# Block fusion on TensorE through diagonal matrices, a larger GpSimd share of the state input product, and two attention steps half a slot away from their old places

## The chip, the cores and the metric

The kernel runs on one core of a Trainium2 chip. The metric is the device time of one execution in microseconds. The core has five engines that run side by side, each through its own instructions in order, and that meet through semaphores: TensorE (PE in the profile; its weight loads are PEld), VectorE (DVE), ScalarE (ACT), GpSimd (POOL) and SyncE (SP), which here issues the DMAs.

## The reference, cut to what matters

The input x has 8 samples of 512 channels by 48 x 48 positions, read as 2304 steps of a sequence, all in fp32. Two layers follow each other.

- Layer 0: group norm, then causal linear attention with 8 heads of 64 channels and features elu + 1; the numerator is divided by the product of Q with the running sum of K; the result is added to x.
- Layer 1: group norm, then four groups of 128 channels, one after the other. Each group runs a Mamba block (projection, convolution over 4 steps, a selective scan with 256 inner channels and 16 states, gating, projection back), and its output is fused with its input. The fused result is added to the input of the next group:

```python
for i in range(4):
    x_i = spx[i] + prev if prev is not None else spx[i]
    x_m = mamba(x_i)
    fused_global = maximum(x_i, x_m)
    w_local, w_global = sigmoid(mean(x_i)), sigmoid(mean(fused_global))
    fused = w_local * x_i + w_global * fused_global
    feats.append(fused); prev = fused
```

The means run over all positions, so a group must be finished before its fusion can start. The concatenated `feats` are added to the input of layer 1. "Block fusion" below means the line of `fused`, and the sum that makes the next group's `x_i`.

## The kernel before

**Blocks, jobs, slots.** A block is one group of one sample (32 blocks). Two streams (`streams[0]` with the even samples, `streams[1]` with the odd ones) take turns block by block, so that the fusion and the preparation of one stream's next block happen while the other stream's block is scanned. A block has 6 chunks of 384 steps (`LC`), each a `Job` of 8 slots (`SLOTS`): 2 halves of the inner channels (`h`) by 4 sets of states (`q`). This makes 1536 slots.

**One slot.** `slot(k)` emits the product of B with delta times x for the next slot, four decays (`decay`, L885, Exp on ScalarE, from SBUF into a PSUM bank), four scans on VectorE (`scan`, L895, which read that bank and the product and write `u`), the weighting by C on GpSimd (`weigh`, L908), and the sum over states on TensorE (`gather`, L922, into the bank `yp`). The product is shared: `product` (L875, VectorE) does the columns 0 to `LC - TAIL` of each of 4 row groups, reading B from PSUM, where ScalarE has copied it (`inputs`, L848, `Bp`); `last_product` (L864, GpSimd, emitted two slots ahead) does the last `TAIL` columns, reading B from SBUF. `TAIL` is 128. `u` has 5 buffers. Scans release their banks in program order, and up to three decays (`DEPTH`) are emitted ahead of the scans while banks are free. Six PSUM banks (`spare`) serve the decays and everything else but `yp` and `Bp`.

**The order of the rest.** All engines' programs are written out by one planner. Work beside the scans is a set of generators (`Task`); each `yield when, banks` says from which half slot on, and with how many free PSUM banks, it goes on. `beside(half)` runs twice per slot: half 2k ahead of the slot's first scan, and half 2k + 1 after its second. It first steps the attention tasks (`heads`) that need no bank, then `tasks` (fusion, preparation, finish of a job), then `heads` again. Since the same things come back every job, a period is 8 slots or 16 halves; below, "half 7" means half 7 of such a period.

**Attention** is a second pipeline, `chunk(m)`: one chunk of 384 steps of two heads (`o` is the pair of heads) per period, started at half 3 (`times[m]`, then `at(j)` is j halves later). It projects q (half 3), k (5) and v (7) at L300, each four products; ScalarE makes Exp (L312) and Relu (L313), and VectorE the features q (L359, half 5) and k (L367, half 7). At half 8 TensorE sums k along the sequence (`kc`, L373, plus the sum kept from the pass before, L375, where `o` is not 0), VectorE multiplies with q (`pr`, L386, half 10), and ScalarE copies v and kc (L378, L382, half 9). The states and denominators follow (L405 to L423, half 15); `rd` is 1/denominator (L433), `rdb` its broadcast (L441). In the next period TensorE transposes `rdb` (L445, `at(16)`, half 3), VectorE scales q with it (L450, half 5), TensorE makes the scores of two heads (L457, L467, half 6), ScalarE takes their masked part by a Relu into `sm` (L479, `at(21)`, half 8), TensorE makes the output (L484 to L498, half 9), ScalarE copies it out (L508, half 11). With `o` 0, GpSimd also normalises the input, four times L324.

**Preparation of a job** (`prepare`): convolution (L707) at halves 11 and 13, gate (L718), Silu (L743 to L748) at half 14, then B, C and delta go through DRAM and come back spread over partitions (L797 to L812). GpSimd makes `dx` (L819). The finish of a job, two slots into the next, is `yz` on VectorE (L934), the projection (L940) at half 4, and the maximum (`fg`, L951).

**Fusion** is `Stream.pass_on`. `wt` holds the two sigmoid weights, `xi` the stream's current `x_i` for all steps, `fu` the loaded maximum, `xb` the next group's slice of layer 1's input, `xa` (tile `xo`) the old group's slice. `loads(c)` loads the three. For each chunk ScalarE scales `fu` and `xi` (L668, L669) and normalises `xb` (L673), GpSimd adds `fu` and `xi` (L676), and then `xb`, into `xi` (L681); a third addition makes the output (L684). When the next group belongs to a new sample (`self.fresh`), there is no L681, and ScalarE normalises straight into `xi` (L679). The tasks are placed at 33 and 25 half slots ahead of the job that needs them, the first chunk of a block as soon as its norm is known.

Of the kernel before, what the change touches and what calls it, by code (L numbers as in the profile page):

```python
# [9 lines left out]
F32 = mybir.dt.float32  # L10
BF16 = mybir.dt.bfloat16
AF = mybir.ActivationFunctionType
ALU = mybir.AluOpType
# [4 lines left out]
P = 128  # L18
T = 128
LC = 384  # L20
NI, NQ, NGR = 4, 4, 4
SLOTS = 8
TAIL = 128
BANKS = 6
DEPTH = 3
LEAD = 11
# [23 lines left out]
def attention_then_mamba_kernel(  # L50
# [12 lines left out]
    nc = tc.nc  # L63
    B, _, L = x.shape
    NS = 16
    NC = L // LC
# [6 lines left out]
    small = ctx.enter_context(tc.tile_pool(name="small", bufs=2))  # L73
# [7 lines left out]
    ident = cst[:, C_ID : C_ID + P]  # L81
# [198 lines left out]
    def chunk(m):  # L280


        b, o, c = parts[m]
        n = f"{b}_{o}_{c}"
        bank = Banks()
        NT = LC // T
        cols, tile_rows = slice(c * LC, (c + 1) * LC), slice(o * P, (o + 1) * P)
# [3 lines left out]
        def at(j, gap=1):  # L291
            return times[m] + j, gap
# [23 lines left out]
        if o == 0:  # L316
# [3 lines left out]
            xn, norm = fetched.pop(m), norms[b]  # L320
# [85 lines left out]
        more = NT if c + 1 < NC else NT - 1  # L406
# [4 lines left out]
        if c:  # L411
# [4 lines left out]
                start=True,  # L416
                stop=False,
                skip_group_check=True,
            )
        for i in range(more):  # L420
            for j in range(i + 1):
                for h in heads_of:
# [16 lines left out]
        yield at(15), 0  # L439
        rdb = new("rdb", 1, (P, 2 * NT, 64))  # L440
        nc.scalar.copy(rdb, rd.unsqueeze(2).to_broadcast([P, 2 * NT, 64]))  # L441
        yield at(16), 1
        rb = bank()[:, 0:LC].rearrange("p (i t) -> p i t", i=NT)
        for i in range(NT):
            nc.tensor.transpose(  # L445
# [10 lines left out]
        for sc in scs:  # L456
# [4 lines left out]
                start=True,  # L461
                stop=False,
                skip_group_check=True,
            )
        for i in range(NT):
            for h, sc in zip(heads_of, scs):
# [4 lines left out]
                    start=False,  # L471
                    stop=i == NT - 1,
                    skip_group_check=True,
                )
        yield at(21), 0
        sms = []
        for par, sc in enumerate(scs):
            sm = new(f"sm{par}", 1, (P, NT, T))
# [43 lines left out]
    class Stream:  # L522
# [55 lines left out]
        def pass_on(self):  # L578


            xi = self.xi
            old = None
            if self.b is not None:
                old = self.b, self.s, self.n, self.fm
                wt = small.tile([P, 4], F32, tag="wt", name=f"wt_{self.n}")
                nc.vector.tensor_copy(wt[:, 2:3], self.sums)
                nc.vector.tensor_reduce(wt[:, 3:4], self.fsum, AX.X, ALU.add)
            last = old is not None and old[1] == 3 and not self.samples
            if old is not None:
                yield "1", 0  # L590
                nc.scalar.activation(wt[:, 0:2], wt[:, 2:4], AF.Exp, scale=-1.0 / L)
                yield "1", 0
                nc.vector.tensor_scalar_add(wt[:, 0:2], wt[:, 0:2], 1.0)
                nc.vector.reciprocal(wt[:, 0:2], wt[:, 0:2])
            if not last:
                self.move_on()
                while (self.b, self.s) not in done:
                    yield "1w", 0
                norm = done[self.b, self.s]
            s = self.s  # L600
            if not last:
# [12 lines left out]

            def loads(c):
                fu = xb = xa = None
                cols = slice(c * LC, (c + 1) * LC)
                if not last:
                    xb = mpool.tile([P, LC], F32, tag="xb", name=f"xb_{self.n}_{c}")
                    nc.sync.dma_start(out=xb, in_=x1s[self.b][s * P : (s + 1) * P, cols])  # L620
                if old is not None:
                    fu = mpool.tile([P, LC], F32, tag="fu", name=f"fu_{old[2]}_{c}")
                    nc.sync.dma_start(out=fu, in_=old[3][:, cols])
                    xa = mpool.tile([P, LC], F32, tag="xo", name=f"xo_{old[2]}_{c}")
                    nc.sync.dma_start(out=xa, in_=x1s[old[0]][old[1] * P : (old[1] + 1) * P, cols])
                return fu, xb, xa

            if last and self.z:

                got = [  # L630
                    mpool.tile([P, 4, 1 + LC], F32, tag="u", name=f"end_{i}", bufs=5)
                    for i in range(NC // 2)
                ]
                for c in range(NC):
                    fu, xa = (got[c // 2][:, c % 2 * 2 + i, 0:LC] for i in range(2))
                    cols = slice(c * LC, (c + 1) * LC)
                    rows = slice(old[1] * P, (old[1] + 1) * P)
                    nc.sync.dma_start(out=xa, in_=x1s[old[0]][rows, cols])
                    nc.sync.dma_start(out=fu, in_=old[3][:, cols])
                for c in range(NC):  # L640
                    fu, xa = (got[c // 2][:, c % 2 * 2 + i, 0:LC] for i in range(2))
                    cols, icols = slice(c * LC, (c + 1) * LC), slice(3 + c * LC, 3 + (c + 1) * LC)
                    for t, i in ((xi[:, icols], 0), (fu, 1)):
                        nc.vector.scalar_tensor_tensor(
                            xa, t, wt[:, i : i + 1], xa, ALU.mult, ALU.add
                        )
                    nc.sync.dma_start(out=out[old[0], rows, cols], in_=xa)
                return
            now = loads(0)
            for c in range(NC):  # L650

                if c and not last:
                    first = 2 * self.jobs[self.block * NC + c].start
                    yield (first - 33, 1), 0
                    now = loads(c)
                    yield (first - 25, 1), 0
                elif c:
                    yield "3", 0
                    now = loads(c)
                    yield "1", 0  # L660
                else:
                    yield "1", 0
                cols, icols = slice(c * LC, (c + 1) * LC), slice(3 + c * LC, 3 + (c + 1) * LC)
                fu, xb, xa = now
                if not last:
                    normed = dict(bias=norm[:, 1, :], scale=norm[:, 0, :])
                if old is not None:
                    nc.scalar.activation(fu, fu, AF.Copy, scale=wt[:, 1:2])  # L668
                    nc.scalar.activation(xi[:, icols], xi[:, icols], AF.Copy, scale=wt[:, 0:1])  # L669
                if old is None:  # L670
                    nc.scalar.activation(xi[:, icols], xb, AF.Identity, **normed)
                elif not last and not self.fresh:
                    nc.scalar.activation(xb, xb, AF.Identity, **normed)  # L673
                if old is not None:
                    yield "1", 0
                    nc.gpsimd.tensor_tensor(fu, fu, xi[:, icols], ALU.add)  # L676
                    yield "2" if c and self.fresh and not last else "1", 0
                    if not last and self.fresh:
                        nc.scalar.activation(xi[:, icols], xb, AF.Identity, **normed)  # L679
                    elif not last:  # L680
                        nc.gpsimd.tensor_tensor(xi[:, icols], xb, fu, ALU.add)  # L681
                    self.ready = c + 1
                    yield "1", 0
                    nc.gpsimd.tensor_tensor(xa, xa, fu, ALU.add)  # L684
                    save(out[old[0], old[1] * P : (old[1] + 1) * P, cols], xa)
                self.ready = c + 1

    class Job:

# [281 lines left out]
    for n in range(4 * NC * B):  # L971
        block, c = n // NC, n % NC
# [121 lines left out]
    def at(k):  # L1094
        return jobs[k // SLOTS], k % SLOTS
# [198 lines left out]
```

## Time and profile before

| what | value |
|---|---|
| median of 3 runs | 8326.95 us (8322.77 to 8327.64) |
| profiled execution, its own time | 8326.65 us |
| its span, first to last instruction | 8324.9 us |
| mean granted TensorE clock | 0.931 |
| first scan starts, last scan starts | 193.3, 8300.7 us |
| busy: PE, DVE, ACT, POOL | 7181.1, 7964.6, 7076.7, 7756.5 us |

The span is what the profile's shares refer to; the profiled execution's own time lies 1.75 us above it. In a group of instructions the columns are: line, engine, operation, output <- inputs, shapes, count, then the busy time of the group in us, the mean length of one in ns, and the idle time of the engine ahead of them with what ended most of it. Successive instructions of VectorE overlap by some tens of ns, so busy time over count is less than the mean length. An fp32 matmul has two records. A line of the waits reads: who waited for whom, us in total, times, longest.

### The profile page before, as it was taken

What the parts mean: (1) busy time and instruction counts of PE and PEld (TensorE: products, weight loads), DVE (VectorE), ACT (ScalarE), POOL (GpSimd) and SP (SyncE); (2) the same over time, 40 slices, a digit from 0 to 9 for tenths busy, and PEclk for the clock granted to TensorE, in tenths of its full rate; (3) what the DMA queues carried; (4) which work ended last, traced back from release to release, by engine and by line L of the source; (5) the groups of instructions that cost most, each with busy time, mean ns of one, the idle gap of its engine ahead of it and who ended that gap; (6) DMA issues with size and microseconds to landing.
All of it is one profiled execution on the core that took longest, in us unless ns stands there. A gap on an engine that the chain in (4) does not pass through costs nothing.

```text
span 8324.9 us, 131321 instructions
## 1 busy us (share of the span) xinstructions
PE 7181.1 (86%) x38850; PEld 3392.3 (41%) x38850; DVE 7964.6 (96%) x10534; ACT 7076.7 (85%) x15014; POOL 7756.5 (93%) x4235
## 2 busy tenths in 40 slices
PE   8888888888888888888888888888888888888864
PEld 4444444443344444444444444444434444444421
DVE  3999999999999999999999999999999999999998
ACT  3888888888888888888888888888888888888886
POOL 2989999999999999999999999999999999999998
PEclk9999999999899999999999999999999999999976
DMA  6777878877777887787777778887777777777765
GB/s 202 194 188 200 210 205 206 206 194 202 205 199 200 204 206 206 198 204 197 202 205 200 199 205 208 205 201 195 203 202 205 201 193 201 203 198 196 190 169 145
DMA packets 1097343, 1654.89 MB, mean 199 GB/s; under 512 B 143913, under 2 KB 989353, under 8 KB 1096498
## 3 DMA queue, kind: packets, MB, share of 16 engines
q1 hardware_dynamic: 1096626, 1646.48, 76.9%
q8 instruction: 309, 5.06, 0.3%
q14 instruction: 408, 3.34, 0.1%
HBM read 1318.23 MB, written 327.68 MB: 198 GB/s over the span
## 4 chain that ended last, share of the span: by engine, by line
DVE 30%; ACT 24%; PE 14%; DMA 14%; issue 10%; POOL 5%; SPq 3%; ACTq 0%; DVEq 0%; POOLq 0%
DVE u L895 20%; PE bank L300 9%; ACT bank L885 8%; DVE u L875 6%; POOL u L908 3%; DMA dxr<-xscr 3%; ACT L885 2%; DMA dr<-dscr 2%; DMA B<-scr 2%; ACT L743 2%; DMA xo<-x 2%; ACT L778 1%; PE bank L718 1%; SPq L810 1%; SPq L797 1%
## 5 line engine op out<-in xcount | busy, mean ns | idle before, releaser
L895 DVE TENSOR_TENSOR_SCAN u<-bank,u 128x385 f32<-128x385 f32 (+1 forms) x6144 | 5442.9, 938 | 110.7 <-ACT bank L885 109.1
L908 POOL TENSOR_TENSOR u<-u,C 128x1536 f32<-128x1536 f32 x1536 | 4890.4, 3184 | 365.7 <-DVE u L895 203.7
L885 ACT ACTIVATE bank<-dr,scales 128x385 f32<-128x385 f32 (+1 forms) x6144 | 3399.5, 579 | 558.6 <-DVE u L895 532.1
L864 POOL TENSOR_TENSOR u<-B,dxr 128x512 f32<-128x512 f32 x1536 | 1966.1, 1280 | 28.0 <-DMA ksum<-before 15.4
L300 PE MATMUL bank<-xn,wq 128*128 128x384 f32 x4608 | 1946.3, 573 | 36.5 <-DVE u L895 14.5
L875 DVE TENSOR_TENSOR u<-Bp,dxr 128x1024 f32<-128x1024 f32 x1536 | 1842.9, 1200 | 15.0 <-ACT Bp L848 9.5
L922 PE MATMUL yp<-u,cst 128*32 128x384 f32 x12288 | 1357.7, 514 | 326.8 <-POOL u L908 168.8
L300 PEld LDWEIGHTS bank<-xn,wq 128*128 128x128 f32 x4608 | 971.5, 222 | 932.0 <-issue 252.5
L707 PE MATMUL bank<-xi,wk 128*128 128x384 f32 x3072 | 1102.4, 502 | 184.4 <-ACT xr L508 174.4
L707 PEld LDWEIGHTS bank<-xi,wk 128*128 128x128 f32 x3072 | 557.1, 191 | 749.4 <-issue 172.2
L922 PEld LDWEIGHTS yp<-u,cst 128*32 128x32 f32 x12288 | 255.3, 109 | 985.1 <-POOL u L908 439.7
L312 ACT ACTIVATE ex<-bank,bqkv_sb 128x384 f32<-128x384 f32 x384 | 222.9, 580 | 423.1 <-PE bank L300 423.1
L885 ACT ACT_TABLE_LOAD x382 | 490.1, 1283 | 6.7
L848 ACT COPY Bp<-B 128x512 f32<-128x512 f32 x768 | 450.9, 587 | 26.4 <-DVE u L875 16.0
L718 PE MATMUL bank<-xi,scales 128*128 128x384 f32 x768 | 327.7, 510 | 124.3 <-ACT xs L743 124.3
L819 POOL TENSOR_TENSOR dx<-delta,xs 128x384 f32<-128x384 f32 x384 | 385.5, 1004 | 22.2 <-ACT delta L778 22.2
L445 PE MATMUL bank<-cst,rdb 128*128 128x128 f32 x576 | 138.0, 365 | 268.1 <-DVE u L895 267.5
L767 PE MATMUL bank<-dbc,steps_w 9*128 9x384 f32 x768 | 307.8, 521 | 27.7 <-DVE rd L433 12.7
L940 PE MATMUL bank<-yz,scales 128*128 128x384 f32 x768 | 299.5, 511 | 27.5 <-DVE yz L934 16.3
L754 PE MATMUL bank<-xs,scales 128*40 128x384 f32 x768 | 285.0, 494 | 0.0
L498 PE MATMUL bank<-sm,v 128*64 128x128 f32 x2304 | 256.1, 301 | 0.0
L863 ACT COPY u<-state 128x4 f32<-128x4 f32 x1280 | 249.7, 195 | 0.4
(118 smaller groups left out, 8085.8 us busy)
## 6 DMA issues: line engine op xcount, KB each, us to landing
dr<-dscr SPq DMA_DIRECT2D x1536, 192.0 KB, 4.7
dxr<-xscr SPq DMA_DIRECT2D x1536, 192.0 KB, 5.3
xn<-xn SPq DMA_DIRECT2D x192, 768.0 KB, 5.4
B<-scr SPq DMA_DIRECT2D x1536, 96.0 KB, 4.2
C<-scr SPq DMA_DIRECT2D x1536, 96.0 KB, 3.0
dscr<-delta SPq DMA_DIRECT2D x192, 384.0 KB, 5.0
xscr<-dx SPq DMA_DIRECT2D x192, 384.0 KB, 2.9
xn<-in_x SPq DMA_DIRECT2D x48, 768.0 KB, 5.4
```

Source lines behind the costliest of these rows:

```text
L300: nc.tensor.matmul(ps, wqs[m // NC][:, kt, j * P : (j + 1) * P], xn[:, kt, :], start=(kt == 0), stop=(kt == 3),)
L707: nc.tensor.matmul(xc, wk[:, k, h * P : (h + 1) * P], xi[:, c0 + k : c0 + k + LC], start=(k == 0), stop=(k == 3),)
L718: nc.tensor.matmul(zp, w_gate[:, s, h * P : (h + 1) * P], xi[:, c0 + 3 : c0 + 3 + LC], start=True, stop=True,)
L767: nc.tensor.matmul(vp, steps_w[32:41, s, h * P : (h + 1) * P], dbc[32:41, :], start=True, stop=True)
L819: nc.gpsimd.tensor_tensor(dx[:, h, :], delta[:, h, :], xs[:, h, :], ALU.mult)
L848: nc.scalar.copy(self.Bp, self.B[pair % 2][:, :, 0 : LC - TAIL])
L864: nc.gpsimd.tensor_tensor(u[:, :, 1 + LC - TAIL :], self.B[q // 2][:, q % 2, cols].unsqueeze(1).to_broadcast(shape), self.dxr[h][:, :, col ...
L875: nc.vector.tensor_mul(u[:, :, 1 : 1 + LC - TAIL], self.Bp[:, s % 2, :].unsqueeze(1).to_broadcast(shape), self.dxr[s // NQ][:, :, cols],)
L885: nc.scalar.activation(dA[:, cols], self.dr[h][:, g, cols], AF.Exp, scale=w_a[:, self.w[1], NGR * h + g, q : q + 1],)
L895: nc.vector.tensor_tensor_scan(u[:, g, cols], dA[:, cols], u[:, g, cols], 0.0, ALU.mult, ALU.add,)
L908: nc.gpsimd.tensor_tensor(u[:, :, 0:LC], u[:, :, 1:], self.C[q // 2][:, q % 2, :].unsqueeze(1).to_broadcast([P, NGR, LC]), ALU.mult,)
L922: nc.tensor.matmul(self.yp[g * 32 : g * 32 + 32, 0:LC], state_sum, u[:, g, 0:LC], start=False, stop=s % NQ == NQ - 1, skip_group_check=True,)
```

## The change

- `TAIL` goes from 128 to 152: of the 384 columns of each row group, GpSimd takes 152 and VectorE 232.
- Block fusion: once per block ScalarE makes two or three diagonal 128x128 matrices (`mix`: the identity scaled by w_local, by w_global and, inside a sample, by the norm's scale). For each chunk TensorE multiplies `xi` and `fu` by the first two into one PSUM bank (`mixed`); half a slot later ScalarE copies it to `fu`, and TensorE adds the third matrix times `xb` into the same bank; half a slot later ScalarE writes it with the norm's shift to `xi` and gives the bank free. L668, L669, L673, L676 and L681 go; the addition of L684 stays on GpSimd, half a slot earlier. The last fusion of stream 0 uses the bank too; that of stream 1 stays as it was.
- The first chunk of a block has the same places, 33 and 25 half slots ahead, as the others.
- In `chunk`, the transposes of `rdb` go from `at(16)` to `at(17)`, half 3 to half 4; the Relu of the scores goes from `at(21)` to `at(20)`, half 8 to half 7.

```diff
-TAIL = 128
+TAIL = 152
...
-        yield at(16), 1
+        yield at(17), 1
         rb = bank()[:, 0:LC].rearrange("p (i t) -> p i t", i=NT)
...
-        yield at(21), 0
+        yield at(20), 0
         sms = []
...
-            now = loads(0)
+            if old is not None:
+                mix = small.tile([P, 3, P], F32, tag=f"mix{self.z}", name=f"mix_{old[2]}", bufs=1)
+                factors = [wt[:, 0:1], wt[:, 1:2]]
+                if not last and not self.fresh:
+                    factors.append(norm[:, 0, :])
+                for i, factor in enumerate(factors):
+                    nc.scalar.activation(mix[:, i, :], ident, AF.Copy, scale=factor)
+            now = loads(0) if old is None or last else None
             for c in range(NC):
...
-                if c and not last:
+                if now is None:
                     first = 2 * self.jobs[self.block * NC + c].start
                     yield (first - 33, 1), 0
                     now = loads(c)
-                    yield (first - 25, 1), 0
+                    yield (first - 25, 1), 0 if old is None else 1
...
-                if old is not None:
-                    nc.scalar.activation(fu, fu, AF.Copy, scale=wt[:, 1:2])
-                    nc.scalar.activation(xi[:, icols], xi[:, icols], AF.Copy, scale=wt[:, 0:1])
                 if old is None:
                     nc.scalar.activation(xi[:, icols], xb, AF.Identity, **normed)
-                elif not last and not self.fresh:
-                    nc.scalar.activation(xb, xb, AF.Identity, **normed)
-                if old is not None:
+                else:
+                    bank = Banks()
+                    mixed = bank()[:, 0:LC]
+                    more = len(factors) == 3
+                    for i, src in enumerate((xi[:, icols], fu)):
+                        nc.tensor.matmul(
+                            mixed, mix[:, i, :], src, start=i == 0, stop=i == 1, skip_group_check=True
+                        )
                     yield "1", 0
-                    nc.gpsimd.tensor_tensor(fu, fu, xi[:, icols], ALU.add)
-                    yield "2" if c and self.fresh and not last else "1", 0
-                    if not last and self.fresh:
+                    nc.scalar.copy(fu, mixed)
+                    if more:
+                        nc.tensor.matmul(
+                            mixed, mix[:, 2, :], xb, start=False, stop=True, skip_group_check=True
+                        )
+                    yield "1", 0
+                    if more:
+                        nc.scalar.activation(
+                            xi[:, icols], mixed, AF.Identity, bias=norm[:, 1, :]
+                        )
+                    elif not last:
                         nc.scalar.activation(xi[:, icols], xb, AF.Identity, **normed)
-                    elif not last:
-                        nc.gpsimd.tensor_tensor(xi[:, icols], xb, fu, ALU.add)
+                    bank.free()
                     self.ready = c + 1
-                    yield "1", 0
                     nc.gpsimd.tensor_tensor(xa, xa, fu, ALU.add)
```

More of the change, by code (lines that the diff above doesn't have):

```diff
@@ L648, in pass_on @@
                 return
-            now = loads(0)
+            if old is not None:
[6 more added lines that the diff above has]
+            now = loads(0) if old is None or last else None
             for c in range(NC):
-                if c and not last:
+                cols, icols = slice(c * LC, (c + 1) * LC), slice(3 + c * LC, 3 + (c + 1) * LC)
+                if now is None:
                     first = 2 * self.jobs[self.block * NC + c].start
@@ L655, in pass_on @@
                     now = loads(c)
-                    yield (first - 25, 1), 0
-                elif c:
-                    yield "3", 0
-                    now = loads(c)
-                    yield "1", 0
-                else:
-                    yield "1", 0
-                cols, icols = slice(c * LC, (c + 1) * LC), slice(3 + c * LC, 3 + (c + 1) * LC)
+                    yield (first - 25, 1), 0 if old is None else 1
+                else:
+                    yield "1", 0 if old is None else 1
@@ L664, in pass_on @@
                 fu, xb, xa = now
+                now = None
                 if not last:
                     normed = dict(bias=norm[:, 1, :], scale=norm[:, 0, :])
-                if old is not None:
-                    nc.scalar.activation(fu, fu, AF.Copy, scale=wt[:, 1:2])
-                    nc.scalar.activation(xi[:, icols], xi[:, icols], AF.Copy, scale=wt[:, 0:1])
                 if old is None:
                     nc.scalar.activation(xi[:, icols], xb, AF.Identity, **normed)
-                elif not last and not self.fresh:
-                    nc.scalar.activation(xb, xb, AF.Identity, **normed)
@@ L679, in pass_on @@
                         nc.scalar.activation(xi[:, icols], xb, AF.Identity, **normed)
-                    elif not last:
-                        nc.gpsimd.tensor_tensor(xi[:, icols], xb, fu, ALU.add)
+                    bank.free()
                     self.ready = c + 1
-                    yield "1", 0
                     nc.gpsimd.tensor_tensor(xa, xa, fu, ALU.add)
@@ L686, in pass_on @@
                 self.ready = c + 1
+                if last and c + 1 < NC:
+                    yield "3", 0
+                    now = loads(c + 1)
     class Job:
```

## The prediction

> **What bounds the kernel now.** I read the page first (busy shares, then groups of instructions), then the answer on waits, then the windows of the end, then a timeline of one period in mid-span. The page:
>
> ```profile
> PE 7181.1 (86%) x38850; PEld 3392.3 (41%) x38850; DVE 7964.6 (96%) x10534; ACT 7076.7 (85%) x15014; POOL 7756.5 (93%) x4235
> ...
> L895 DVE TENSOR_TENSOR_SCAN u<-bank,u 128x385 f32<-128x385 f32 (+1 forms) x6144 | 5442.9, 938 | 110.7 <-ACT bank L885 109.1
> L908 POOL TENSOR_TENSOR u<-u,C 128x1536 f32<-128x1536 f32 x1536 | 4890.4, 3184 | 365.7 <-DVE u L895 203.7
> ...
> L864 POOL TENSOR_TENSOR u<-B,dxr 128x512 f32<-128x512 f32 x1536 | 1966.1, 1280 | 28.0 <-DMA ksum<-before 15.4
> ...
> L875 DVE TENSOR_TENSOR u<-Bp,dxr 128x1024 f32<-128x1024 f32 x1536 | 1842.9, 1200 | 15.0 <-ACT Bp L848 9.5
> ```
>
> DVE and POOL are both nearly full. Which one leads is told by who waits for whom: GpSimd's weighting (L908) stood idle 203.7 us for DVE's scans, while DVE's waits, next fence, name ScalarE and almost never GpSimd. So DVE sets the pace. A plain slot costs DVE four scans of 5442.9/6144 = 0.886 us and one product of 1.200 us, 4.74 us in all, and GpSimd 3.184 + 1.280 = 4.46 us; the rest of the mean slot of some 5.28 us (first scan at 193.3, last at 8300.7, 1536 slots) is other work.
>
> ```profile
> DVE u L895 <- ACT bank L885: 109.1, 147, 4.8
> DVE q L359 <- ACT bank L313: 76.3, 94, 5.4
> ...
> DVE u L895 <- POOL u L864: 1.3, 1, 1.3
> ```
>
> The exception is the end, where no attention is left for DVE to do. In these windows (columns PE, PEld, DVE, ACT, POOL busy, clock, DMA) GpSimd is the fuller engine:
>
> ```profile
> 7900.00:8100.00 200.00, 139.76 (x612) 53.23 (x612) 194.20 (x239) 161.58 (x336) 196.28 (x106) 0.74 0.68 168
> 8100.00:8325.00 225.00, 110.81 (x440) 31.75 (x440) 195.67 (x236) 144.28 (x315) 201.42 (x107) 0.61 0.59 148
> ```
>
> [...] (1200 - 545)/(1024 - 384) = 1.02 ns per element between L875 and L386. [...] (3184 - 1280)/1024 = 1.86 ns, and I take that. [...] the product is even (1191 to 1226 ns), so the two prices may be used side by side. [...]
>
> **The change part by part.** The sum is made against the profiled execution, 8326.65 us (span 8324.9 and 1.75 around it), 0.3 below the median shown.
>
> *TAIL 128 to 152.* Each product moves 4 x 24 = 96 elements from DVE to GpSimd. DVE: 1536 x 96 x 1.02 ns = **-151 us**, on the path. GpSimd: 1536 x 96 x 1.86 = +274 us. ScalarE's copy Bp loses 48 elements, about 0.04 us x 768 = -31 us.
>
> *Fusion.* GpSimd loses L676 (186, 187.0 us) and L681 (144, 144.7 us), 332 us; L684 stays. GpSimd ends at -58 us. ScalarE loses L668, L669 and L673, 114.6 + 112.6 + 100.5 = 328 us; it gains 186 copies like L508 (0.476), 144 activations from PSUM like L378 (0.572) and 86 diagonal matrices of 128x128 (some 0.31), 198 us. With Bp it ends at -161 us. This is no gain on the path where ScalarE only waits for scans (532 us of such waits). No DMA is added; the three loads of each group's first chunk move by a few half slots, onto the place that the other chunks have, and SP keeps its order but for neighbouring issues (loads of C, xn and before around them) and output stores, each a few places off.
>
> TensorE gets 186 pairs and 144 third products. No row shows them; the nearest are L300, four 128x384 products in a row in 2.85 us (0.71 each), and L940, 0.91 alone. Pair 1.62, third 0.81: 301 + 117 = **+418 us of TensorE**, about 2.2 us per chunk, all in halves 7 and 8 of the 16 of a period. Queued behind: the v projection, then the running key sum kc, then DVE's pr (L386) and ScalarE's copies L378 and L382. In the timeline further below kc would move from about 4032.7 to 4035.0, and past another 0.7 us of L375 where o > 0; pr runs at 4036.85. It nearly fits. Bounds: -10 us (pr waits 15.6 today) to +60; I take +10. The third product waits for a ScalarE copy (0.48 us) issued in the same half, but stands behind 2.85 us of v projection, which hides it. The pair holds a PSUM bank for two halves, taken by the Relu step now freeing two banks earlier, so decays keep theirs.
>
> *Relu a half earlier (21 to 20).* It takes away TensorE's wait of kc for the Relu's banks, 171.9 us of weight load and 70.9 of matmul; DVE doesn't see that. Its own cover is ScalarE's spare; if the scores are late, decays queue behind it. Counted at nothing, in the bounds above.
>
> *Denominator's transposes a half later (16 to 17).* Today L445 stands ahead of the q projection in TensorE's queue and waits for a bank that a scan gives free:
>
> ```profile
> PE bank L445 <- DVE u L895: 267.5, 177, 3.1
> PEld bank L373 <- ACT sm L479: 171.9, 183, 3.9
> ```
>
> The timeline of one period, in order of time (start, length, engine, line):
>
> ```profile
> 4014.93 0.90 PE L445 MATMUL bank<-cst,rdb 128*128 128x128 f32 x3
> 4015.62 3.43 PE L300 MATMUL bank<-xn,wq 128*128 128x384 f32 x8
> ...
> 4021.09 0.91 PE L940 MATMUL bank<-yz,scales 128*128 128x384 f32 x2 [0.67 <-DVE yz L934]
> ...
> 4022.67 0.53 DVE L450 TENSOR_TENSOR q<-q,bank 128x384 f32<-128x384 f32 x1
> ...
> 4032.66 0.91 PE L373 MATMUL bank<-k,cst 128*128 128x384 f32 x2 [0.45 <-ACT sm L479]
> ...
> 4036.85 0.55 DVE L386 TENSOR_TENSOR pr<-q,bank 128x384 f32<-128x384 f32 x1
> ```
>
> Moved, the q projection starts up to 1.5 us sooner and DVE's wait at L359 goes: of 76.3 us I count **-50**, the rest lying ahead of the first scan. What is late next is L450: the order of instructions puts L445 behind L940, whose second product waits for DVE's yz. L940 ends at 4022.00, and 0.90 more is 4022.9, against 4022.67 where DVE wants it: 0.2 us, over 184 chunks, **+32** (bounds 0 to 60). The k projection takes the bank that L450 frees, so k slips with it: +10 (0 to 20).
>
> *Where the 151 us do not arrive.* From about 7900 on, some 80 slots, GpSimd binds: 8 us of it don't count, and GpSimd's own sum there is about even (80 x 0.178 = +14 against 18 fusion operations of 1.0). In the 48 chunks of a sample's first attention pass GpSimd also has four L324 (2.7 us), and a fresh group's fusion takes away only one addition: there it comes to some 42.8 us a period, about DVE's own; +12. Together **+20**. Once a period ScalarE's burst of four Silu and two table loads ends the wait (DVE's wait for decays, 109.1 us); a product 0.1 us shorter inside it meets the same burst: **+13**.
>
> Sum: -151 + 20 - 50 + 32 + 10 + 10 + 13 = -116, so **8211 us**.
>
> **The rivals.**
> (B) The new waits hide: no +32, +10, +10, +13, and half of the decays' 109 us goes with ScalarE's lighter load: 8326.65 - 151 - 50 + 20 - 55 = 8091. For it: ScalarE loses 161 us. Against: the timeline's slack at L450 is already negative.
> (C) GpSimd becomes the bound everywhere: its idle after the first 200 us (568.4 - 156.9 = 411.5) stays and only its -58 us shows: 8269. For it: 93% full, and 0.178 us more in every slot. Against: last_product runs a slot ahead of its scan, and DVE waits 1.3 us for it today.
> (D) The new waits eat the saving (kc at its upper 60, L450 at its 60, k 20): about 8310 to 8343.
> (E) **Slower: TensorE becomes the bound.** Between 200 and 7900 us it is busy 6766 and idle 934. L445's and L373's matmul waits (338 us) go, 596 stay; 6766 + 410 + 596 = 7772 against 7700, so 8399. It decides in halves 7 to 9, from the point where the remaining waits shrink by less than 72 us. For it: [...] busy 7176 of 7600 us. Against: most of these waits are TensorE ahead of others (for GpSimd's weighted states, for ScalarE's copies), and shrink when it runs late; a stream of products also takes 0.71 where lone ones take 0.91.
> That the change fails to act is excluded: DVE's product does have 928 elements.
>
> **How the numbers follow.** My forecast (8160 to 8260) 0.52, B (8080 to 8160) 0.17, C (8250 to 8310) 0.12, D 0.06, E (8343 to 8420) 0.13. Faster by over 0.2%, about what a measurement of this kernel can tell: A, B, C, 0.81; within it D, 0.06; slower E, 0.13. The range 8085 to 8340 leaves out E and a sliver of B.
>
> **What would show it.** Right: L875 at about 1.10 us, L864 at 1.46, DVE busy near 7815, the wait at L359 all but gone, a new one at L450 of some 30 us, PE near 7600. Wrong: waits of DVE on L864 in the hundreds (C); waits at L386, or at decays behind L382 or the new activation, above 100 us (D, E); TensorE's idle below 5% (E).

## The result, and the profile after

| | before | after |
|---|---|---|
| median time | 8327.3 us (8322.77 to 8332.12) | **8283.49 us** (8280.25 to 8289.05, 4 runs) |
| ratio, 95% interval | | 0.9948 [0.9931, 0.9965], -43.8 us |
| span of the profiled execution | 8324.9 us | 8282.2 us |
| mean granted TensorE clock | 0.931 | 0.944 |

Faster, by a little over a third of the 116 us forecast, and inside the range. Lines after the fusion are 15 higher in the changed kernel: the scan is L910 (it was L895), VectorE's product L890 (L875), GpSimd's L879 (L864), the decays L900 (L885), the gather L937 (L922), `yz` L949 (L934), the projection back L955 (L940). L300 to L479 keep their numbers. New on TensorE are the pair (L678) and the third product (L684).

The page of the changed kernel, busy shares and groups, with the columns of before:

```profile
PE 7354.5 (89%) x39882; PEld 3572.9 (43%) x39882; DVE 7829.1 (95%) x10534; ACT 6991.8 (84%) x14914; POOL 7753.9 (94%) x3905
...
L910 DVE TENSOR_TENSOR_SCAN u<-bank,u 128x385 f32<-128x385 f32 (+1 forms) x6144 | 5447.2, 939 | 115.2 <-ACT bank L900 112.9
L923 POOL TENSOR_TENSOR u<-u,C 128x1536 f32<-128x1536 f32 x1536 | 4894.5, 3187 | 349.1 <-DVE u L910 210.3
L879 POOL TENSOR_TENSOR u<-B,dxr 128x608 f32<-128x608 f32 x1536 | 2286.1, 1488 | 14.5 <-DMA x<-xr 13.8
L890 DVE TENSOR_TENSOR u<-Bp,dxr 128x928 f32<-128x928 f32 x1536 | 1690.2, 1100 | 10.9 <-ACT Bp L863 7.2
```

VectorE's product fell from 1200 to 1100 ns and its group by 1842.9 - 1690.2 = 152.7 us, as worked out. GpSimd is as full as before, and its weighting still waits for VectorE (210.3 us): it did not become the bound, though its lateness reaches VectorE by a detour in some chunks (experiment 5). The answer lies in VectorE's waits (for whom, us in total, times, longest):

```profile
DVE q L450 <- PE bank L445: 143.2, 129, 4.2
DVE u L910 <- ACT bank L900: 112.9, 137, 4.8
DVE pr L386 <- ACT before L382: 30.9, 66, 4.2
...
DVE q L359 <- ACT bank L313: 23.5, 9, 6.6
...
DVE yz L949 <- PE yp L937: 18.0, 35, 5.3
```

VectorE is busy 135.5 us less (7964.6 to 7829.1) and idle 92.8 us more. The idle part by groups: L450 +140.8, L359 -54.9, L367 -17.6, `pr` +15.3, `yz` +9.5, scans +4.5. Two thirds of the saving became waits, and nearly all of it is one wait that came in place of another: VectorE no longer waits for the q projection's activations, it waits for the transposes of `rdb`.

Where that time goes is in TensorE's waits of the changed kernel:

```profile
PE bank L678 <- ACT sm L479: 241.4, 173, 1.9
PE bank L300 <- DVE u L910: 233.4, 180, 2.9
```

The first is new: the fusion's pair waits for a bank that the Relu gives free. The second is the old one. The wait of 267.5 us that L445 had for a scan's bank is now ahead of L300, the q projection, in nearly the same size. It was handed on, not removed. One period of the changed kernel, TensorE (start, length, line, then idle time before it in brackets):

```profile
3521.08 0.85 PE L937 MATMUL yp<-u,cst 128*32 128x384 f32 x8 [0.30 <-POOL u L923]
3523.29 4.54 PE L300 MATMUL bank<-xn,wq 128*128 128x384 f32 x8 [1.36 <-DVE u L910]
3527.66 1.45 PE L955 MATMUL bank<-yz,scales 128*128 128x384 f32 x4
3528.95 0.49 PE L445 MATMUL bank<-cst,rdb 128*128 128x128 f32 x3
...
3530.41 2.85 PE L300 MATMUL bank<-xn,wq 128*128 128x384 f32 x8
```

and VectorE in the same period:

```profile
3527.18 1.80 DVE L910 TENSOR_TENSOR_SCAN u<-bank,u 128x385 f32<-128x385 f32 x2
3529.48 0.56 DVE L450 TENSOR_TENSOR q<-q,bank 128x384 f32<-128x384 f32 x1 [0.50 <-PE bank L445]
```

The q projection takes 4.54 us, the k projection, the same four products, 2.85. The windows of this stretch say why (length, PE, PEld, DVE, ACT, POOL busy, then the granted clock, DMA):

```profile
3519.90:3523.30 3.40, 1.74 (x12) 0.35 (x10) 3.40 (x5) 3.35 (x9) 3.40 (x3) 1.00 0.92 229
3523.30:3526.70 3.40, 3.40 (x6) 1.87 (x7) 3.40 (x4) 3.36 (x5) 3.40 (x2) 0.50 0.91 285
3526.70:3530.10 3.40, 3.22 (x19) 1.72 (x17) 2.90 (x6) 3.40 (x10) 3.40 (x2) 0.99 0.98 345
```

In the 3.40 us ahead of the q projection TensorE is busy for half the time (1.74 us), and for the next 3.40 us it runs at half clock (0.50). Over the whole kernel the q projection has a median of 4.54 us and is above 3.2 us in 72% of the chunks. It was no faster before (4.43 us, 96%), but then L445 stood ahead of it and L450 did not need it. Now L445 follows it and L955, so VectorE pays for the slow projection.

### The profile page after: what moved, and what is told of

The parts are those of the page before. It is cut to its first block, busy times and chain, and to the rows that moved or that the text cites. A ratio compares the mean times of both kernels' runs of the same rounds, so it can differ in the third digit from the quotient of the medians.

```text
span 8282.2 us, 133009 instructions
## 1 busy us (share of the span) xinstructions
PE 7354.5 (89%) x39882; PEld 3572.9 (43%) x39882; DVE 7829.1 (95%) x10534; ACT 6991.8 (84%) x14914; POOL 7753.9 (94%) x3905
## 5 line engine op out<-in xcount | busy, mean ns | idle before, releaser
L910 DVE TENSOR_TENSOR_SCAN u<-bank,u 128x385 f32<-128x385 f32 (+1 forms) x6144 | 5447.2, 939 | 115.2 <-ACT bank L900 112.9
L923 POOL TENSOR_TENSOR u<-u,C 128x1536 f32<-128x1536 f32 x1536 | 4894.5, 3187 | 349.1 <-DVE u L910 210.3
L900 ACT ACTIVATE bank<-dr,scales 128x385 f32<-128x385 f32 (+1 forms) x6144 | 3414.1, 579 | 612.8 <-DVE u L910 574.6
L879 POOL TENSOR_TENSOR u<-B,dxr 128x608 f32<-128x608 f32 x1536 | 2286.1, 1488 | 14.5 <-DMA x<-xr 13.8
L300 PE MATMUL bank<-xn,wq 128*128 128x384 f32 x4608 | 1886.5, 558 | 286.1 <-DVE u L910 233.4
L890 DVE TENSOR_TENSOR u<-Bp,dxr 128x928 f32<-128x928 f32 x1536 | 1690.2, 1100 | 10.9 <-ACT Bp L863 7.2
L937 PE MATMUL yp<-u,cst 128*32 128x384 f32 x12288 | 1353.7, 513 | 200.8 <-POOL u L923 122.8
L300 PEld LDWEIGHTS bank<-xn,wq 128*128 128x128 f32 x4608 | 955.4, 216 | 1189.5 <-DVE u L910 373.4
L937 PEld LDWEIGHTS yp<-u,cst 128*32 128x32 f32 x12288 | 249.1, 109 | 776.7 <-issue 415.7
L863 ACT COPY Bp<-B 128x464 f32<-128x464 f32 x768 | 420.5, 548 | 21.3 <-DVE u L890 13.1
L678 PE MATMUL bank<-xi,mix 128*128 128x384 f32 x372 | 175.4, 554 | 249.6 <-ACT sm L479 241.4
L955 PE MATMUL bank<-yz,scales 128*128 128x384 f32 x768 | 329.1, 541 | 51.3 <-DVE yz L949 41.7
L782 PE MATMUL bank<-dbc,steps_w 9*128 9x384 f32 x768 | 306.4, 519 | 22.3 <-DVE rd L433 17.6
L733 PE MATMUL bank<-xi,scales 128*128 128x384 f32 x768 | 296.3, 496 | 18.9 <-ACT xs L758 18.8
L498 PE MATMUL bank<-sm,v 128*64 128x128 f32 x2304 | 254.7, 299 | 0.0
```

The source lines that it names most:

```text
L300: nc.tensor.matmul(ps, wqs[m // NC][:, kt, j * P : (j + 1) * P], xn[:, kt, :], start=(kt == 0), stop=(kt == 3),)
L782: nc.tensor.matmul(vp, steps_w[32:41, s, h * P : (h + 1) * P], dbc[32:41, :], start=True, stop=True)
L863: nc.scalar.copy(self.Bp, self.B[pair % 2][:, :, 0 : LC - TAIL])
L879: nc.gpsimd.tensor_tensor(u[:, :, 1 + LC - TAIL :], self.B[q // 2][:, q % 2, cols].unsqueeze(1).to_broadcast(shape), self.dxr[h][:, :, col ...
L890: nc.vector.tensor_mul(u[:, :, 1 : 1 + LC - TAIL], self.Bp[:, s % 2, :].unsqueeze(1).to_broadcast(shape), self.dxr[s // NQ][:, :, cols],)
L900: nc.scalar.activation(dA[:, cols], self.dr[h][:, g, cols], AF.Exp, scale=w_a[:, self.w[1], NGR * h + g, q : q + 1],)
```

## The experiments

**What is tested.** First: the lost time is the transposes' new place in TensorE's queue. Rivals: the larger share of GpSimd or the fusion makes the lateness, and the move of the transposes is harmless (the prediction's -8). Second, once that stood: the transposes are late because the q projection ahead of them runs at half clock. Rival: only the order counts, whatever the clock.

All times are medians; the ratio behind each is against the kernel before, measured beside it on the same chip: 8326.1 us for experiments 1 to 4, 8329.3 for 5 to 8 and 8325.4 for 9 to 12.

**1. Transposes back at half 3** (changed kernel)

```diff
-        yield at(17), 1
+        yield at(16), 1
         rb = bank()[:, 0:LC].rearrange("p (i t) -> p i t", i=NT)
```

> The changed kernel with the denominator's transposes back at half 3 (at(16)), all else kept. Theory Q (the missing 73 us is VectorE's new wait at L450, made by TensorE's order: q projection, then L955's two products, then L445): L450's wait falls from 143 us to under 10, and the wait at L359 comes back to 50 to 80 us; 8195 to 8235 us. Theory T (TensorE is late in general from the added fusion products, the order of these three does not matter): L450's wait falls, but waits of the same size appear at L359, L367 and the decays; 8265 to 8300.

8236.98 us (8232.29 to 8240.86), 0.9892 [0.9877, 0.9906]: 46.5 us faster than the changed kernel. The wait at L450 is down to 2.4 us, and the one at L359 is back:

```profile
DVE u L910 <- ACT bank L900: 113.3, 135, 4.3
DVE q L359 <- ACT bank L313: 87.6, 118, 6.6
DVE pr L386 <- ACT before L382: 38.5, 65, 4.7
```

The time lies 2 us above the range expected, and L359 takes back a little more than the 80 us at most. So the move of the transposes, which the prediction priced at -8 us, costs 46 us here.

**2. The projection back (L955) out of the way of the transposes**

```diff
-        yield "0", 1
+        yield "2", 1
```

> The changed kernel with the finish of a job (the projection L955) one half slot later, so that L445 stands directly behind the q projection and L955 behind it; transposes stay at half 4. Theory Q: L450's wait falls to under 40 us and L359's stays small; k's wait at L367 or fg's may rise by up to 30; 8170 to 8215 us. Theory T: L450's wait stays above 100 us, or the same sum shows at L367 and L966; 8265 to 8300. A third possibility, the bank wait of the q projection (233 us at L300 in TensorE) being the cause alone: L450 keeps about half of its 143 us; about 8220.

8521.03 us, 1.0233 [1.0218, 1.0249]. The wait at L450 fell to 34.2 us as wanted, and another took its place: in the new order the k features are late.

```profile
DVE k L367 <- ACT bank L313: 180.5, 190, 3.7
DVE u L910 <- ACT bank L900: 118.4, 139, 3.9
DVE yz L949 <- PE yp L937: 49.5, 48, 5.0
```

The time is a miss: 238 us above the changed kernel, of which VectorE's idle time explains 139 and its busy time 97. A step moved by half a slot is no small test here; it shows that L955 had to do with L450, and not what L450 would cost by itself.

**3. TAIL back to 128** (changed kernel, `-TAIL = 152`, `+TAIL = 128`)

> The changed kernel with TAIL back at 128; fusion on TensorE and both moves kept. If the 1536 x 0.1 us of VectorE's product came through in full, this takes 8283 + 130 to 155 = 8415 to 8440 us, slower than the kernel before. If GpSimd already eats part of the saving, 8340 to 8390. The wait at L450 stays near 140 us or falls a little, as VectorE comes there 0.1 us later per product.

8364.16 us (8356.13 to 8365.44), 1.0043 [1.0028, 1.0058]. With the transposes at half 4, the kernel without the larger share is slower than before, and the share is worth 81 us of the 148.6 by which VectorE's product grows. The wait at L450 is 134.9 us: its sum does not come from `TAIL`, though one part of it does (experiment 5).

**4. The Relu back at half 8** (changed kernel)

```diff
-        yield at(20), 0
+        yield at(21), 0
         sms = []
```

> The changed kernel with the Relu of the scores back at half 8 (at(21)). Theory Q: little to VectorE, the v projection and kc come half a slot later on TensorE as the fusion's bank is another; pr's wait rises from 31 us to 40 to 100; 8283 to 8345 us. Theory T: TensorE, late already, gets later: 8330 us or more. If the earlier Relu costs (ScalarE waits for scores), this is faster, 8250 to 8280.

8903.04 us (8890 to 8922), 1.0693 [1.0675, 1.0711]: a miss by far. VectorE's waits, then one of TensorE's:

```profile
DVE pr L386 <- ACT before L382: 497.7, 133, 7.1
DVE pr L386 <- PE bank L375: 193.0, 48, 5.2
DVE q L450 <- PE bank L445: 132.4, 111, 4.2
```

```profile
PE bank L684 <- ACT fu L682: 285.2, 143, 4.8
```

ScalarE's copy of the mixed bank (L682) is issued in the same half as the Relu and stands behind it, and the third product waits for the copy. TensorE's order changes too: in 137 of the 144 periods with a third product the v projection now stands behind it instead of ahead, and the key sum `kc` behind the output products (L484 to L498) as well. `kc` starts 6.3 us (median) after the third product's end, where in the changed kernel it follows at once, and `pr` waits for `kc`. This fits the two banks of the scores being given free half a slot later, so that none is free for v and `kc` at their old places. The step that the prediction counted at nothing is what makes the fusion, placed as it is here, fit.

**5. TensorE kept busy ahead of the q projection** (changed kernel). Six 128x128 products per chunk, which nothing reads, into unused columns of `yp`, behind the broadcast of `rd` at half 2:

```diff
         nc.scalar.copy(rdb, rd.unsqueeze(2).to_broadcast([P, 2 * NT, 64]))
+        for _ in range(6):
+            nc.tensor.matmul(
+                yp[:, LC:512], ident, ident, start=False, stop=False, skip_group_check=True
+            )
```

> The changed kernel plus six 128x128 fp32 products of the identity per chunk into 128 columns of the bank yp that nothing reads, in TensorE's queue ahead of the last gather of a job (half 2), so that TensorE is busy where it idles ahead of the q projection. Theory C (clock): in the changed kernel the q projection runs at the halved clock that the records show for 3.4 us behind that idle stretch (4.5 us where k and v take 2.85), and L445 stands behind it; with the stretch filled it takes 2.9 us, the wait at L450 falls from 143 us to under 50, and the time to 8165 to 8215 us. Theory O (order alone: L445 is late because L955 waits for yz in front of it): the wait at L450 stays above 110; 8265 to 8310 us. If the products only delay what is behind them: 8300 us or more.

8220.09 us (8212.48 to 8228.04), 0.9869 [0.9854, 0.9883]: 63 us faster than the changed kernel, by work that is thrown away. The mean granted clock is 0.975, time at half clock falls from 934 us to 421, and the median of the q projection from 4.54 to 2.85 us. L450 (now L454) waits 44 times instead of 129:

```profile
DVE u L914 <- ACT bank L904: 114.5, 138, 6.0
DVE q L454 <- PE bank L449: 94.3, 44, 7.1
```

The time lies 5 us above the range expected, and the 94.3 us that stay at L450 are more than the 50. Each wait matched to the q projection ahead of it tells why. In the chunks of the later passes (`o` not 0, 144 of 192) the wait at L450 falls from 75.4 us in 87 places to 3.7 us in 3: there the theory of the clock holds. In the 48 chunks of the first pass, where GpSimd normalises the input of the projection (L324), it does not fall (65.3 us in the changed kernel, 88.9 here). In 35 of these chunks, with 76.1 us of the wait, the q projection itself stood still for GpSimd for more than 0.3 us. TensorE's waits:

```profile
PE bank L300 <- POOL xn L324: 74.6, 36, 2.9
```

In the changed kernel such chunks have 51.3 of the 143.2 us, and with `TAIL` 128 (experiment 3) 5.5 of the 134.9. So the larger share does make VectorE wait there, not for GpSimd's product but through `xn`, the q projection and the transposes. That these waits come from L324 is read from the traces; no experiment took them away.

**6. Both: transposes at half 3, and the six products** (edits 1 and 5)

> The transposes back at half 3, and the same six filling products. Theory C: the q projection is at full clock, the 88 us of wait at L359 of the run with the transposes at half 3 fall to under 30; 8165 to 8200 us, better than both kernels. Theory O: L359 keeps its 88 us, as the q projection is late by the transposes' wait for a bank ahead of it; 8230 to 8260 us.

8193.59 us (8191.65 to 8201.48), 0.9839 [0.9824, 0.9853]. Faster than either alone, 1.6% under before. L359 waits 59.6 us in 43 places (87.6 in 118 without the products): part of the price at the old place was also the clock. The wait was to fall under 30; 57.6 us of what stays lie in the chunks of the first pass.

**7. TAIL 152 alone** (kernel before)

> The kernel before with TAIL 152 alone. If GpSimd, with its 332 us of fusion additions still there, becomes the bound, its 7756 busy grow by 320 to 8076, and with the 411 us of idle after the first 200 and the 157 ahead of it the time is at most 8644; with the idle shrinking, 8330 to 8450 us, slower, with VectorE waiting for L864 by 100 us or more. If VectorE still leads: 8200 to 8270 us.

8394.1 us (8378.74 to 8398.4), 1.0074 [1.0059, 1.0089]. The larger share without the fusion costs 65 us. GpSimd is busy 8056.9 us (96%). The expected wait of VectorE for GpSimd's product does not appear; waits grow in other places (`dxr` is loaded from GpSimd's `dx`):

```profile
DVE u L895 <- ACT bank L885: 147.4, 154, 5.7
DVE q L359 <- ACT bank L313: 123.1, 112, 6.0
DVE u L875 <- DMA dxr<-xscr: 35.7, 34, 1.9
...
DVE norm_m L211 <- POOL norm_m L207: 20.9, 15, 2.4
```

and one small operation of VectorE is longer, from 553 ns before to

```profile
L593 DVE TENSOR_SCALAR wt<-wt 128x2 f32<-128x2 f32 x32 | 68.4, 2137 | 0.3 <-ACT wt L591 0.3
```

**8. Fusion and earlier Relu alone** (changed kernel with edits 1 and 3)

> Fusion on TensorE and the earlier Relu, but TAIL 128 and the transposes at half 3. Set beside the changed kernel with TAIL 128 (8364 us) it tells the cost of the later transposes by another pair: 8310 to 8325 us. If fusion in itself brought VectorE something, this is under 8300; if it costs, over 8335.

8279.71 us (8275.73 to 8282.47), 0.994 [0.9923, 0.9956]: -49.6 us, under the 8300 that was to show a gain of the fusion. Fusion and earlier Relu together are worth something by themselves: decays wait 83.9 us instead of 109.1, k 12.0 instead of 31.1.

**9. The transposes alone at half 4** (kernel before, `at(16)` to `at(17)`)

> The kernel before with one edit, the transposes of rdb half a slot later (half 4). The terms of the prediction for this step alone are -50 at L359, +32 at L450 and +10 for k: about -8, so 8320. The theory of the bank wait handed on to a q projection at half clock says that L445 loses its wait of 267.5 us, L300 gains it, and DVE waits for L450 over 100 us: 8360 to 8415 (the step cost 46 us with the fusion and 152 columns, 84 with 128 columns). A value within 15 us of 8327 would say that the step is bad only beside the fusion.

8396.86 us (8393.17 to 8398.67), 1.0085 [1.0068, 1.0102]: 71.5 us slower. The bank wait is at L300 (261.9 us), and VectorE has

```profile
DVE q L450 <- PE bank L445: 147.4, 155, 4.2
DVE u L895 <- ACT bank L885: 96.5, 137, 3.1
DVE k L367 <- ACT bank L313: 25.6, 18, 3.7
```

The wait needs no fusion.

**10. The six products in the kernel before**

> The kernel before with six products of 128x128 per chunk that nothing reads, behind the broadcast of rd at half 2. Theory of the clock: its half-clock stretches (1156 us in all) become few, the q projection falls from 4.43 to about 2.85 us, DVE's wait at L359 (76.3 us) falls below 50: 8270 to 8305. Rival: L445 stands ahead of the q projection here and DVE never waited for the slow projection itself, so it changes nothing: 8315 to 8340.

8290.9 us (8284.17 to 8298.74), 0.9958 [0.9943, 0.9973]: 34.5 us faster, with time at half clock 482 us instead of 1156, and L359 waiting 38.6 us instead of 76.3. The slow projection cost the kernel before something too.

**11. The same six products at the wrong place** (changed kernel, behind `pr` at half 10 instead of half 2)

> The changed kernel with the same six unread products per chunk, but issued behind pr at half 10, where TensorE is busy anyway. If the gain of the products at half 2 was the clock of the q projection, nothing of it shows here: half-clock time stays near 934 us, the wait at L450 near 143 us, time 8275 to 8300. Rival: any shift of TensorE's order would have done it (the products merely change when banks and copies meet): below 8255.

8493.47 us, 1.0201 [1.0186, 1.0217]. What the theory of the clock said of the clock holds: it stays low (0.939, 1030 us at half clock), and L450 (here L454) waits 151.6 us. That any shift of TensorE's order would do is refuted by this one; other shifts were not tried. The expected time is missed by 200 us, for a reason of its own. TensorE's timeline, then VectorE's:

```profile
3634.10 0.44 PE L502 MATMUL bank<-sm,v 128*64 128x128 f32 x4
3634.47 1.60 PE L389 MATMUL yp<-cst 128*128 128x128 f32 x12
3635.91 0.49 PE L397 MATMUL bank<-cst,k 128*128 128x128 f32 x3
3636.24 0.49 PE L397 MATMUL bank<-cst,vT 128*128 128x128 f32 x3
3636.66 0.85 PE L941 MATMUL yp<-u,cst 128*32 128x384 f32 x8
```

```profile
3637.58 0.56 DVE L953 TENSOR_TENSOR yz<-yp,sz 128x384 f32<-128x384 f32 x1 [1.71 <-PE yp L941]
```

From the pair at half 7 on TensorE works without a gap, and the 1.60 us push the last gather before `yz` past the time VectorE wants it: 211.5 us of waits in 171 places, about the 210 us lost. In this part of the period TensorE has nothing to spare.

**12. The best so far with TAIL 144** (edits 1 and 5)

> Fusion, earlier Relu, transposes at their old half 3 and the six products at half 2, with GpSimd's share 144 columns instead of 152. A third of the way back to 128: if the 24 columns' net 43 us is spread evenly, +14 on 8193.6, so 8208 (8200 to 8215). Rival: the last columns only lengthen the small operations behind GpSimd and the decays' waits, the best size lies below 152: 8180 to 8192.

8186.67 us (8181.83 to 8188.56), 0.9832 [0.9817, 0.9847]. 8208 was expected; the time lies in the range of the rival and is not to be told from 8193.59, as the intervals of the ratios overlap. The last 8 columns bring nothing that could be told: VectorE's busy time grows by 30.6 us, but decays, `pr`, L359 and the small operations take less. This kernel and that of experiment 6 are faster than both kernels of the study.

The parts of the change put together (us):

| | TAIL 128, old fusion | TAIL 128, new fusion and Relu | TAIL 152, new fusion and Relu |
|---|---|---|---|
| transposes at half 3 | 8327 | 8280 | 8237 |
| transposes at half 4 | 8397 | 8364 | 8283 |

TAIL 152 with the old fusion and the transposes at half 3 is 8394. The move of the transposes costs 71, 84 or 46 us by what stands beside it; the fusion, with the Relu, saves 47 or 33; the larger share saves 43 or 81 with the new fusion and costs 67 with the old. The earlier Relu without the fusion was not run, so these two are not told apart.

## Why the prediction was right or wrong

**The failing step is the denominator's transposes.** They were counted at -50 (L359), +32 (L450) and +10 (k), together -8. Alone they cost 71.5 us (experiment 9), beside the rest of the change 46 (experiment 1). With 71.5 in place of -8 the same sum gives -116 + 79 = -37, or 8290 us, near the 8283.5 measured; that it comes so near is luck, as two other errors nearly cancel (below). Of the three terms, L359 was right in size (76.3 to 23.5, -53; part of it may be covered by the wait at L450, directly ahead of it on VectorE), k went the other way (31.1 to 13.5), and **L450 was mis-sized: 32 counted, bound 60, 143.2 measured.**

The working took L450's lateness from one period, and not from a usual one. There the second product of L940 waits for `yz`; in the 182 periods of the trace before whose records are complete, that happens 3 times. In the others L940 starts as the q projection ends, a median of 1.0 us after `yz`, so the q projection decides when L940 ends. The working's own difference, L940's end plus 0.90 us less the start of L450, is 0.2 us in the period quoted and 1.75 us in the mean of the 182. (0.2 us over 184 chunks would also be 37 us and not 32.)

Two things about the q projection were missed. First, it was to start up to 1.5 us sooner. But the wait of 267.5 us was for a free bank, and whoever comes next in the queue takes it over; only the transposes' own time ahead of it went. Against the end of `yz` it starts 0.7 us sooner (3.23 us ahead of it before, 3.97 after, medians). Second, its length: 3.43 us in the period quoted, a median of 4.43, where the next projections take 2.85. The difference is the half clock: in the kernel before, the 9 q projections that lie in no half-clock stretch have a median of 2.85 us too. The lateness adds up over the late chunks alone: 129 of them, 1.1 us each. In the first pass GpSimd's L324 adds its part (experiment 5), a lateness that the prediction named only as +12 for VectorE's product.

**Right:** the product on VectorE (-151 counted, -152.7), its durations (1.10 us, 1094 to 1126 ns; GpSimd's 1.488 for 1.46), the two prices side by side (the scan's mean is 939 ns for 938 before), VectorE's busy time (7829 for 7815), the end of the wait at L359, and that VectorE stays the bound: it never waits on GpSimd's product. `pr` was sized right (+10, measured +15.3), though only thanks to the earlier Relu. ScalarE's new and lost groups came as worked out (202.6 us gained for 198, with 0.39 us for a diagonal matrix instead of 0.31; 327.7 lost for 328; Bp 450.9 to 420.5, -30.4 for -31), but its busy time fell by 84.9 us and not by 161.

**Wrong, and hidden by each other.** The fusion and the Relu were counted at +10 for `pr` and nothing else; they bring -47 to -50 (experiment 8), an error of nearly -60. The larger share was counted at -151 + 33 = -118; at the old place of the transposes it brings -43 (experiments 8 and 1), an error of +75. Between those two kernels the product falls 156.5 us, and back come, among others, the decays' wait (+29), `pr` (+15), `yz` (+14), L593 (+11) and another small operation of VectorE, `gm` (+10). This is rival D's course, in smaller pieces than it named (and D's own terms add up to 8299 us, not to 8310 or more). The two errors nearly cancel, which is why the one bad step explains the miss in the sum.

**GpSimd** ends at -2.6 us instead of -58. The 96 elements cost 208 ns, 2.17 ns each, where I took 1.86 from the difference between two different operations (L908 and L864). More columns of the same operation cost as much in experiment 12: 2.19 ns, (1420 - 1280)/64. It did not decide the time.

**The Relu**, counted at nothing with "ScalarE's spare" as cover, is the dearest step of all beside the fusion: without it +620 us (experiment 4). The prediction saw that it gives two banks free earlier, and counted them for the decays alone; it did not ask which other instructions, the v projection and `kc`, then keep their places.

**TensorE.** The fusion's groups are 448.5 us (418 counted), yet TensorE's busy time grows only by 173.4 (7181.1 to 7354.5), since other groups take less (L300 -59.8, L445 -40.9, L718 -31.4, L373 -17.6 among them), which goes with the time at half clock, 1156 us before and 934 after. So rival E's sum was wrong on the whole, and its place right: in halves 7 to 10 TensorE has no slack left (experiment 11). Rival B (waits hide) and C (GpSimd the bound; its 8269 is near, but its wait on L864 never shows) fall by their mechanisms, C with the exception of the chunks of the first pass.

**Open:** what L324's lateness in the first pass costs by itself; the Relu without the fusion; the decays' wait of some 110 us, which no experiment touched by itself; sizes of `TAIL` other than 128, 144 and 152.

## What to carry to other kernels

A wait for a free buffer belongs to a place in the queue: take the waiting instruction away and the next one takes over the wait (267.5 us at L445 became 233.4 at L300), so work out the new order with the wait still in it, and ask who reads what comes behind. Take a duration from its distribution over all periods, not from one line of a timeline, and where equal products have unequal lengths (4.54 and 2.85 us here) look at the granted clock beside them (0.50). A small step in a full period has to be priced by undoing it alone: here the one counted at nothing was worth 620 us beside the fusion, and the larger share changed sign with its neighbours.

## What the runs showed of the hardware

- **Half clock, in stretches on one grid.** In the kernel before, 206 stretches (median 3.41 us, 1156 us in all) ran at half clock, and 183 of the 192 q projections lie in part in one; 96% of the 192 took over 3.2 us. All 206, and all 156 of the changed kernel (934 us), start within 10 ns of one grid of 3.4133 us that runs through the whole execution. In the changed kernel 133 q projections lie in part in a stretch; the other 59 have a median of 2.85 us. The stretch of TensorE shown ahead of one has no gap above 1.4 us and a busy share of 51%. Of the grid's windows at full clock in which TensorE was busy for 98% or more, 944 before and 1364 after, none was followed by one at half clock; of those busy for 40 to 50%, 98 of 109 before and 10 of 39 after. So the busy share alone does not tell which windows are slowed, and these traces do not show what does. One record of the projections (a product has two) takes 485 to 1009 ns (shortest, median and longest for L300 in the changed kernel):

```profile
L300 PE MATMUL bank<-xn,wq x4608: 485/486/1009, 26.1 to 7878.6; 128*128 128x384 f32 x192
```

- **Thrown-away products paid here.** Six small ones per chunk in the idle stretch brought 34 us in the kernel before (experiment 10), 63 in the changed one (5) and 43 with the transposes at half 3 (6 against 1); in a full stretch the same six cost 210 (11).
- **A tiny VectorE operation can take microseconds.** L593 works on 128x2 elements; its mean is 422 ns at the shortest (experiment 3), 553 before, 2137 in experiment 7 and 3489 in experiment 2. All 48 of those above 1 us in experiments 2 and 7 end 21 to 31 ns after a GpSimd instruction does, some after the second or third that ran beside them. What makes them long was not tested.
